# Attention on one core: some projections computed in halves over two steps, the others moved

## Chip, cores and metric

The kernel runs on one core of a Trainium2 chip. The metric is the device time of one execution in microseconds, taken as the median of several runs.

## The reference

The input is x, 8 sequences of 512 rows of 512 numbers, float32 throughout. A layer of attention and a gated layer stand one after the other, each between two layer normalisations and with a residual:

```python
x = x + layernorm(attention(layernorm(x)))
x = x + layernorm(ffn(layernorm(x)))
# attention: 16 heads of 32
c_kv = x @ W_dkv + b_dkv                  # 512 -> 128 ("ckv")
v = c_kv @ W_uv + b_uv                    # values
c_q = x @ W_dq + b_dq                     # 512 -> 128 ("cq")
q = rotary(c_q @ W_qr + b_qr)             # queries
k = rotary(x @ W_kr + b_kr)               # keys
out = softmax(q k^T / sqrt(32)) v @ W_o + b_o
# ffn: Hadamard transform, up and gate projection, silu, Hadamard transform, W_down
```

## The kernel before

The kernel has two phases. Attention takes the first 916 us of the profiled execution and the gated layer the rest. The change touches attention alone.

**Work by batches and steps.** A batch is one of the 8 sequences (number b). Its 16 heads form 4 groups of 4, and its 512 keys 4 chunks of 128, so that a batch has 16 steps i = 4 x group + c, and attention 128 steps t. The loop over t stands in the source in the order in which each engine then works; no scheduler reorders it. In every step PE does the following:

1. `scores_t(n, c)`: two tiles t (each 128 x 1024, two banks of PSUM) with the transposed scores of one key chunk for the four heads of group n. First come four short bfloat16 matmuls that lay down the rows' biases (L564), then four float32 ones of queries and keys (L573). ACT turns each tile into exponentials p (L585).
2. `weigh` of the step before: exponentials by values, into ops (L606).
3. In the last step of a group (i = 3, 7, 11, 15) `bias_rows` of the next group: four small transposes ps_b (L550), which ACT copies; the second exponential of such a step stands behind that copy.
4. In the third step of a group (i = 2, 6, 10, 14) `sums`: the columns of the exponentials are added up, into l (L623).
5. A piece of the table `BETWEEN`, if the step has one.
6. `row_max` for the step six steps later: two tiles s (L527), of which DVE takes maxima (L535).
7. Another piece, of the table `BEHIND`.

The pieces prepare the next batch (offset 1 in a table's entry), the one after (2), the present one (0) or finish the last (-1): `x_flip` transposes normalised x into xT; `compress` makes cq or ckv from xT by four matmuls of 512 columns; `key` makes one of four key blocks by four such matmuls; `query` and `value` make a block by one matmul each; `out_proj` makes a block of the output by five; `fold` applies a 128 x 128 Hadamard matrix to a sixteenth of W_down by one matmul. `fold_load` reads that sixteenth from memory, DVE does four further levels of the transform in later steps (`levels`), and a DMA writes it back. The steps in `FOLDS` do a fold, those in `READ` load one.

**What keys and queries need afterwards.** ACT copies the product with its bias into lin (L416). At the next call of `turn`, in the step that follows, DVE shuffles lin into rot (L420) and POOL does two products and a sum (L421 to L423). POOL also adds up pairs of exponentials in the second and fourth step of each group (`add_up`, L594), splits the maxima (`split`), takes powers of variances (`inverse_std`, L104 and L105) and adds residuals (L694). DVE adds the pairs' sums in each group's first step (`add_pairs`, L599).

**Buffers.** [...] The pool ps_s has three tiles of two banks, tag s, which `row_max` and `scores_t` take in turn: s, s, t, t in each step. One bank belongs to ops. One bank, ps_f with tag f, serves everything else: bias rows, sums, transposes and all pieces, one after the other. `bank(wide, name)` gives a piece a tile of ps_s if `wide` is set and the bank f otherwise:

```python
if wide or end:
    return ps_s.tile([P, 2, S], F32, tag="s", name=name)[:, 0, :]
return ps_f.tile([P, S], F32, tag="f", name=name)
```

In the steps of `TWO` the piece of `BETWEEN` is not done ahead of `row_max` but behind it, just ahead of the piece of `BEHIND`, and with `wide` set. The first batch has tables of its own (`FIRST_BETWEEN`, `FIRST_BEHIND`), since part of its work is done before the loop and nothing has to be finished. The last batch does the first steps of the gated layer's input instead of preparing a successor (`ENTRY`, `in_step`: fxt, L195, and fxh, L207).

Over the steps, `early` and `later` place the normalisation of x (ACT), its load (SP, step 4), statistics (DVE, steps 6 to 9) and shift (DVE, step 11), and the output's statistics, shift, residual and store.

The pieces of a batch before, by step (in the tables of all batches but the first):

| step | ahead of row_max | behind row_max |
|---|---|---|
| 0, 1 | x_flip 1, x_flip 2 | value 2, key 3 |
| 2, 3 | | query 3, value 3 |
| 4 | x_flip 3 | fold |
| 5, 6 | | cq, key 0 |
| 7 | | out_proj 0 |
| 8, 9, 10 | | query 0 + out_proj 1, query 1 + out_proj 2, fold + out_proj 3 |
| 11, 12 | | key 1, query 2 + ckv |
| 13 | x_flip 0 | value 0 |
| 14, 15 | | key 2, value 1 |

Of the kernel before, what the change touches and what calls it, by code (L numbers as in the profile page):

```python
# [10 lines left out]
F32 = mybir.dt.float32  # L11
BF16 = mybir.dt.bfloat16
I32 = mybir.dt.int32
AF = mybir.ActivationFunctionType
# [3 lines left out]
P = 128  # L18
NB, S, D = 8, 512, 512
DH, GH = 32, 4  # L20
NK = D // P
NT = S // P
INTER = 2048
NI = INTER // P
# [4 lines left out]
C_BDKV, C_BDQ, C_BKR, C_BQR = 0, 1, 2, 6  # L29
# [4 lines left out]
def sandwich_kernel(  # L34
# [19 lines left out]
    nc = tc.nc  # L54
# [17 lines left out]
    pv = const.tile([P, C_END], F32, name="pv")  # L72
    nc.gpsimd.dma_start(out=pv, in_=pvec)
    h128 = const.tile([P, P], F32, name="h128")
# [18 lines left out]
    qkv = ctx.enter_context(tc.tile_pool(name="a_qkv", bufs=2))  # L93
# [148 lines left out]
    with ExitStack() as actx:  # L242
        wa = actx.enter_context(tc.tile_pool(name="wa", bufs=1))
        row = actx.enter_context(tc.tile_pool(name="a_row", bufs=4))
        cproj = actx.enter_context(tc.tile_pool(name="a_c", bufs=1))
        rp = actx.enter_context(tc.tile_pool(name="a_rope", bufs=3))
        pp = actx.enter_context(tc.tile_pool(name="a_p", bufs=1))
        fo = actx.enter_context(tc.tile_pool(name="a_fold", bufs=1))
# [41 lines left out]
        wdkv_sb = wa.tile([P, NK, P], F32, name="wdkv_sb")  # L290
        wdq_sb = wa.tile([P, NK, P], F32, name="wdq_sb")
# [26 lines left out]
        def bank(wide, name):  # L318
# [3 lines that stand above are left out]
# [60 lines left out]
        def x_norm(b, t):  # L382
            rs, sh = stats[b]
            xn[b, t] = row.tile([P, D], F32, tag="xn", name=f"xn_{b}_{t}", bufs=3)
            nc.scalar.activation(
                xn[b, t], xs[b][:, t, :], AF.Identity, bias=sh[:, t : t + 1], scale=rs[:, t : t + 1]
            )
# [26 lines left out]
        def rotate(dst, ps, bias, scale, name, first=None, second=None):  # L414
            lin = rp.tile([P, S], F32, tag="lin", name=f"lin_{name}")
            nc.scalar.activation(lin, ps, AF.Identity, bias=bias, scale=scale)  # L416

            def rest():
                rot = rp.tile([P, S], F32, tag="rot", name=f"rot_{name}", bufs=2)
                nc.vector.stream_shuffle(rot, lin, swap)  # L420
                (first or nc.gpsimd).tensor_mul(lin, lin, cs[:, 0, :])  # L421
                (second or nc.gpsimd).tensor_mul(rot, rot, cs[:, 1, :])
                (first or nc.gpsimd).tensor_add(dst, lin, rot)  # L423

            turns.append(rest)
# [53 lines left out]
            )  # L479
            folds.append((n, w))  # L480

        def fold(n, wide=False):
            _, w = folds.pop(0)
            ps = bank(wide, f"fd_{n}").rearrange("p (c m) -> p c m", c=NI)
            nc.tensor.matmul(ps, lhsT=h128, rhs=w, start=True, stop=True)
            z = fo.tile([P, NI, NF], F32, tag="z", name=f"fz_{n}")
            a = fo.tile([P, NI, NF], F32, tag="a", name=f"fa_{n}")
            nc.scalar.copy(z, ps)

            def level(src, dst, h):  # L490
                sv = src.rearrange("p (a t b) n -> p a t (b n)", t=2, b=h)
                dv = dst.rearrange("p (a t b) n -> p a t (b n)", t=2, b=h)
                nc.vector.tensor_add(dv[:, :, 0, :], sv[:, :, 0, :], sv[:, :, 1, :])
                nc.vector.tensor_sub(dv[:, :, 1, :], sv[:, :, 0, :], sv[:, :, 1, :])

            def keep():
                nc.sync.dma_start(
                    out=wdd.rearrange("p (c m) -> p c m", c=NI)[:, :, ts(n, NF)], in_=w
                )

            levels.extend(
                [
                    lambda: level(z, a, 1),
                    lambda: level(a, z, 2),
                    lambda: level(z, a, 4),
                    lambda: level(a, w, 8),
                    keep,
                ]
            )

        levels = []


        brow, nms, pt, o_ps, o_sb, rec = {}, {}, {}, {}, {}, {}
# [245 lines left out]
        for t in range(3):  # L760
# [11 lines left out]


        BETWEEN = {
            0: (x_flip, 1, 1), 1: (x_flip, 1, 2), 4: (x_flip, 1, 3),
            8: (query, 1, 0), 9: (query, 1, 1), 12: (query, 1, 2), 13: (x_flip, 2, 0),
        }
        BEHIND = {
            0: (value, 0, 2), 1: (key, 0, 3), 2: (query, 0, 3), 3: (value, 0, 3),
            5: (compress, 1, "cq"), 6: (key, 1, 0), 7: (out_proj, -1, 0),  # L780
            8: (out_proj, -1, 1), 9: (out_proj, -1, 2), 10: (out_proj, -1, 3),
            11: (key, 1, 1), 12: (compress, 1, "ckv"), 13: (value, 1, 0), 14: (key, 1, 2),
            15: (value, 1, 1),
        }

        FIRST_BETWEEN = {i: p for i, p in BETWEEN.items() if i not in (8, 9)}
        FIRST_BEHIND = {
            **BEHIND, 7: (query, 1, 0), 8: (None, NB, None), 9: (key, 1, 1),
            10: (None, NB, None), 11: (query, 1, 1),
        }  # L790
        OUT = {7: 0, 8: 1, 9: 2, 10: 3}

        APART = {n: (0, 2) for n in range(NG - NK, NG - 2)}
        APART[NG - 2], APART[NG - 1] = (0, 2, 3), (0, 1, 2, 3)

        FOLDS = [4, 10, 15] + [NK * NT * b + i for b in range(1, NB - 1) for i in (4, 10)]
        FOLDS.append(NK * NT * (NB - 1) + 1)
        READ = [0] + [g - 3 for g in FOLDS[1:]]


        TWO = (8, 9, 10, 12, 15)

        def piece(table, b, i, wide=False):
            if b == 0 and table is BEHIND and i == 8:
                out_bias()
            pieces = table if b else FIRST_BETWEEN if table is BETWEEN else FIRST_BEHIND
            if i in pieces:
                fn, d, what = pieces[i]
                if 0 <= b + d < NB:
                    fn(b + d, what, *([True] if wide else []))  # L810
            at = NK * NT * b + i
            if at in FOLDS and (table is BETWEEN) == (b > 0 and i in TWO or i == 15 or b == NB - 1):
                fold(FOLDS.index(at), wide)
            if b == NB - 1 and (i, table is BEHIND) in ENTRY:
                in_step(*ENTRY[i, table is BEHIND], 2 * NT)

# [17 lines left out]
        def early(b, i):  # L834

            if b > 0 and i - 3 in OUT:
                residual(b - 1, OUT[i - 3])
            if b + 2 < NB and i in (12, 14, 15):
                x_norm(b + 2, max(i - 13, 0))
            if i == 0 and 0 < b + 1 < NB:  # L840
                x_norm(b + 1, 3)

        def later(b, i):

            if b > 0 and i - 1 in OUT:
                out_stats(b - 1, OUT[i - 1])
            if b > 0 and i - 2 in OUT:
                out_shift(b - 1, OUT[i - 2])
            if b > 0 and i - 5 in OUT:
                store(b - 1, OUT[i - 5])  # L850
            if b + 2 < NB:
                if i == 4:
                    load_x(b + 2, NT)
                elif 6 <= i < 10:
                    x_stats(b + 2, i - 6)
                elif i == 11:
                    x_shift(b + 2)

        for t in range(NG * NT):
# [755 lines left out]
```

## Time and profile before

| what | value |
|---|---|
| median of 3 runs | 2101.72 us (2101.01 to 2101.88) |
| profiled execution | 2102.66 us, span 2100.9 us |
| granted TensorE clock | 0.999 |
| attention, from the first step to the gated layer | 46.8 to 916.3 us |
| batch 0 | 102.1 us |
| each of batches 1 to 5 | 108.6 to 108.7 us |
| batch 6 | 108.1 us |
| last batch and end of attention | 116.0 us |

The lengths of the batches are those of the windows in which I asked the trace for busy time; each begins with the first bias matmul (L564) of a batch. PE is TensorE's matmuls and PEld its loads of weights, DVE is VectorE, ACT ScalarE, POOL GpSimd and SP the engine that issues DMAs. A float32 matmul appears as two instructions in the trace, so a key block of four matmuls is "x8". The lengths of single matmuls include a tail of the pipeline in which the next one already runs; the chain of waits gives the time from one to the next.

### The profile page before, as it was taken

How to read it: one execution, taken by the hardware profiler on the slowest of the kernel's cores; microseconds unless marked ns; L12 is line 12 of the kernel's file. 1: busy time of each engine (PE TensorE's matmuls, PEld its weight loads, DVE VectorE, ACT ScalarE, POOL GpSimd, SP SyncE). 2: the span in 40 equal slices, each digit the busy share in tenths (PEclk: the TensorE clock that was granted, in tenths of full speed). 3: DMA queues.
4: the chain of work that ended last, by engine and by line, in shares of the span. 5: the costliest groups of instructions: out<-in, count | busy, mean ns of one | idle time of the engine just before them, and what ended most of it. 6: DMA issues, size and time to landing. Idle time of an engine off the chain costs nothing.

```text
span 2100.9 us, 26741 instructions
## 1 busy us (share of the span) xinstructions
PE 2076.8 (99%) x9035; PEld 1057.4 (50%) x9042; DVE 1414.4 (67%) x2356; ACT 745.3 (35%) x1199; POOL 1575.4 (75%) x1629
## 2 busy tenths in 40 slices
PE   8999999999999999999999999999999999999998
PEld 4333333333333333344444677676676766777753
DVE  5698777676767677465545866678866678656542
ACT  3554545555555545522121122222222222222211
POOL 4787979787878889645453678788888879787852
PEclk9999999999999999999999999999999999999999
DMA  3112121212121122237454444444343344444432
GB/s 122 37 31 51 42 54 49 47 51 52 46 57 46 32 66 72 70 104 221 145 166 152 146 143 148 133 138 149 130 157 131 131 137 144 138 158 136 138 112 70
DMA packets 215913, 218.12 MB, mean 104 GB/s; under 512 B 87376, under 2 KB 147920, under 8 KB 215776
## 3 DMA queue, kind: packets, MB, share of 16 engines
q1 hardware_dynamic: 215424, 215.32, 33.2%
q8 instruction: 72, 1.18, 0.2%
q0 software_dynamic: 352, 1.08, 0.1%
q14 instruction: 65, 0.53, 0.1%
HBM read 169.18 MB, written 46.92 MB: 103 GB/s over the span
## 4 chain that ended last, share of the span: by engine, by line
PE 94%; DVE 3%; issue 1%; POOL 1%; ACT 1%; DMA 0%; SPq 0%; POOLq 0%; DVEq 0%; ACTq 0%
PE d L1123 24%; PE psy L1225 18%; PE s L527 6%; PE ops L606 6%; PE ps_k L439 5%; PE ps_y L662 5%; PE t L573 5%; PE u L1106 5%; PE g L1106 4%; PE psz L1516 3%; PE t L564 3%; PE l L623 2%; PE ps_q L454 2%; PE ps_v L466 1%; PE ps_cq L407 1%; PE fxh L207 1%
## 5 line engine op out<-in xcount | busy, mean ns | idle before, releaser
L1225 PE MATMUL psy<-wd,g 128*128 128x512 f32 x896 | 448.9, 592 | 0.0
L535 DVE TENSOR_REDUCE nm<-s 128x2 f32<-128x1024 f32 x256 | 300.8, 1216 | 175.1 <-PE s L527 175.1
L1347 POOL TENSOR_TENSOR pr<-pr,pr 128x512 f32<-128x512 f32 x294 | 391.6, 1357 | 9.0
L594 POOL TENSOR_TENSOR p<-p,p 128x512 f32<-128x512 f32 x244 | 330.2, 1384 | 22.1 <-PE ops L606 22.1
L585 ACT ACTIVATE p<-t 128x1024 f32<-128x1024 f32 x256 | 251.8, 1023 | 89.0 <-PE t L573 89.0
L1123 PE MATMUL d<-xb,wq 128*128 128x256 f32 x992 | 254.2, 380 | 1.9 <-DVE inner L1139 1.4
L1123 PEld LDWEIGHTS d<-tt,wq 128*128 128x128 f32 x864 | 164.0, 190 | 144.4 <-issue 106.0
L1123 PE MATMUL d<-tt,wq 128*128 128x256 f32 x864 | 233.8, 379 | 0.2 <-DVE pr L1144 0.2
L1140 POOL TENSOR_TENSOR pr<-inner 128x256 f32<-128x256 f32 x168 | 126.0, 750 | 138.5 <-DVE inner L1139 105.9
L1123 PEld LDWEIGHTS d<-xb,wq 128*128 128x128 f32 x992 | 186.7, 190 | 62.4 <-issue 30.1
L1225 PEld LDWEIGHTS psy<-wd,g 128*128 128x128 f32 x896 | 169.7, 190 | 49.3 <-issue 29.4
L1136 ACT COPY inner<-d 128x256 f32<-128x256 f32 x168 | 62.6, 373 | 309.6 <-PE d L1123 291.5
L1132 ACT COPY inner<-d 128x256 f32<-128x256 f32 x168 | 62.6, 372 | 300.3 <-PE d L1123 193.2
L527 PE MATMUL s<-kT,qT 32*128 32x512 f32 x1024 | 153.8, 639 | 0.7 <-DVE nm L535 0.7
L573 PE MATMUL t<-qT,kT 32*128 32x512 f32 x1024 | 142.8, 598 | 0.0
L606 PE MATMUL ops<-p,v 128*32 128x512 f32 x1024 | 136.8, 605 | 0.0
L1142 POOL TENSOR_TENSOR pr<-pr,inner 128x256 f32<-128x256 f32 x168 | 136.5, 813 | 0.0
L1123 PE MATMUL d<-T,wq 128*128 128x256 f32 x496 | 127.6, 380 | 0.2
L1144 DVE TENSOR_TENSOR pr<-d,inner 128x256 f32<-128x256 f32 x168 | 70.5, 420 | 75.5 <-PE d L1123 72.9
L439 PE MATMUL ps_k<-xT,wkr_sb 128*128 128x512 f32 x256 | 118.3, 605 | 0.7 <-ACT xT L397 0.7
L662 PE MATMUL ps_y<-wo_sb,oT 128*128 128x512 f32 x256 | 115.8, 593 | 0.9 <-DVE oT L657 0.6
L1135 DVE TENSOR_TENSOR inner<-d,inner 128x256 f32<-128x256 f32 x168 | 70.5, 419 | 62.4 <-PE d L1123 62.0
(219 smaller groups left out, 3263.8 us busy)
## 6 DMA issues: line engine op xcount, KB each, us to landing
wq<-wdeep SPq DMA_DIRECT2D x168, 448.0 KB, 4.2
wd<-wdd SPq DMA_DIRECT2D x112, 256.0 KB, 2.8
wdeep<-w SPq DMA_DIRECT2D x32, 448.0 KB, 5.5
xr<-in_x SPq DMA_DIRECT2D x32, 256.0 KB, 2.8
xin<-x1d SPq DMA_DIRECT2D x32, 256.0 KB, 4.0
xres<-x1d SPq DMA_DIRECT2D x32, 256.0 KB, 3.3
out<-fy SPq DMA_DIRECT2D x32, 256.0 KB, 2.0
rec<-rd SPq DMA_DIRECT2D x124, 64.0 KB, 2.0
```

The lines of the kernel that those rows point to most:

```text
L439: nc.tensor.matmul(ps, lhsT=wkr_sb[:, k, ts(g, P)], rhs=xT[b][:, k, :], start=(k == 0), stop=(k == NK - 1),)
L527: nc.tensor.matmul(sp[j // 2][:, j % 2, :], lhsT=qT[b][rows, g, ts(qc, P)], rhs=kT[b][rows, g, :], start=True, stop=True,)
L535: nc.vector.tensor_reduce(nms[n][:, qc, 2 * h : 2 * h + 2], sp[h], AX.X, ALU.max, negate=True)
L573: nc.tensor.matmul(sp[j // 2][:, j % 2, :], lhsT=kT[b][rows, g, ts(c, P)], rhs=qT[b][rows, g, :], start=False, stop=True,)
L585: nc.scalar.activation(pt[n, c, h], sp[h], AF.Exp)
L594: nc.gpsimd.tensor_add(into, into, pt[n, c, j // 2][:, j % 2, :])
L606: nc.tensor.matmul(o_ps[n][j * DH : (j + 1) * DH, :], lhsT=vv[b][:, c, ds(g * P + j * DH, DH)], rhs=pt[n, c, j // 2][:, j % 2, :], start=( ...
L662: nc.tensor.matmul(ps, lhsT=oT[b][:, k, ts(qc, P)], rhs=wo_sb[:, k, :], start=False, stop=(k == NK - 1),)
L1106: nc.tensor.matmul(ps, lhsT=w[:, SLOT[n], k, :], rhs=rhs[:, k, :], start=k == 0, stop=k == 1)
L1123: nc.tensor.matmul(ps, lhsT=w[:, INNER[m]], rhs=rhs[m], start=True, stop=True)
L1225: nc.tensor.matmul(ys_[t], lhsT=g[:, ts(t, P)], rhs=w, start=n == 0, stop=n == NI - 1)
L1347: nc.gpsimd.tensor_add(pr[n][:, h], pr[a][:, h], pr[b][:, h])
```

## The change

In every batch but parts of the first and last, the pieces are laid out anew:

| steps | ahead of row_max | behind row_max |
|---|---|---|
| 15 and 0 | x_flip 2 (step 0) | halves of value 1 and key 3 |
| 1 and 2 | x_flip 3 (step 1) | halves of value 2 and cq |
| 3 and 4 | | halves of value 3 and key 0 |
| 5 and 6 | | halves of a fold and key 1 |
| 7, 8, 9, 10 | | query 0 to 3, each with out_proj 0 to 3 |
| 11 and 12 | x_flip 0 (step 12) | halves of a fold and ckv |
| 13 and 14 | x_flip 1 (step 13) | halves of value 0 and key 2 |

`halves` takes the one bank f for a step. Its first 256 columns hold one half of the small piece (one matmul of 256 columns), the other 256 one half of the large piece (four such matmuls); then ACT copies the two out one after the other. After the second half the key's rotation or the fold's levels are queued as before. Where only one piece of a pair is left, in the last batch, it is done whole in the first of the two steps.

The normalisation of x moves from steps 12, 14, 15 to 11, 12, 14, its shift from 11 to 10, the loads of the folds by one step. `TWO` is now 7, 8, 9, 10, 15. In the first batch halves begin at step 13; queries 1, 2 and 3 are done in steps 9, 11 and 10. In the last batch value 2 is done in step 1 and the fold in step 2.

```diff
         def rotate(dst, ps, bias, scale, name, first=None, second=None):
             lin = rp.tile([P, S], F32, tag="lin", name=f"lin_{name}")
             nc.scalar.activation(lin, ps, AF.Identity, bias=bias, scale=scale)
+            rotation(dst, lin, name, first, second)
+
+        def rotation(dst, lin, name, first=None, second=None):
             def rest():
...
+        HC = S // 2
+        split_in_two = {}
+
+        def half(h, ps, fn, b, what):
+            cols = ts(h, HC)
+            if fn is fold:
...
+                nc.tensor.matmul(pv_, lhsT=h128, rhs=w[:, blocks, :], start=True, stop=True)
+                def leave():
+                    nc.scalar.copy(z[:, blocks, :], pv_)
+                    if h == 1:
+                        folds.pop(0)
+                        fold_levels(n, w, z)
+                return leave
+            if fn is value:
...
+                nc.tensor.matmul(
+                    ps, lhsT=cT[b, "ckv"][:, ts(what, P)], rhs=wuv_sb[:, cols], start=True, stop=True
+                )
+                return lambda: nc.scalar.copy(vv[b][:, what, cols], ps)
...
+            for k in range(NK):
+                nc.tensor.matmul(
+                    ps, lhsT=w[:, k, :], rhs=xT[b][:, k, cols], start=k == 0, stop=k == NK - 1
+                )
+            def leave():
+                nc.scalar.activation(dst[:, cols], ps, AF.Identity, bias=bias)
+                if fn is key and h == 1:
+                    rotation(kT[b][:, what, :], dst, f"k{b}_{what}")
+            return leave
...
         BETWEEN = {
-            0: (x_flip, 1, 1), 1: (x_flip, 1, 2), 4: (x_flip, 1, 3),
-            8: (query, 1, 0), 9: (query, 1, 1), 12: (query, 1, 2), 13: (x_flip, 2, 0),
+            0: (x_flip, 1, 2), 1: (x_flip, 1, 3), 7: (query, 1, 0), 8: (query, 1, 1),
+            9: (query, 1, 2), 10: (query, 1, 3), 12: (x_flip, 2, 0), 13: (x_flip, 2, 1),
         }
-        BEHIND = {
+        BEHIND = {7: (out_proj, -1, 0), 8: (out_proj, -1, 1), 9: (out_proj, -1, 2), 10: (out_proj, -1, 3)}
+        HALVES = {
+            15: ((value, 1, 1), (key, 1, 3)), 1: ((value, 0, 2), (compress, 1, "cq")),
+            3: ((value, 0, 3), (key, 1, 0)), 5: ((fold, 0, None), (key, 1, 1)),
+            11: ((fold, 0, None), (compress, 1, "ckv")), 13: ((value, 1, 0), (key, 1, 2)),
+        }
+        FIRST_BETWEEN = {
+            0: (x_flip, 1, 1), 1: (x_flip, 1, 2), 4: (x_flip, 1, 3), 9: (query, 1, 1),
+            10: (query, 1, 3), 12: (x_flip, 2, 0), 13: (x_flip, 2, 1),
+        }
+        FIRST_BEHIND = {
             0: (value, 0, 2), 1: (key, 0, 3), 2: (query, 0, 3), 3: (value, 0, 3),
...
+            5: (compress, 1, "cq"), 6: (key, 1, 0), 7: (query, 1, 0), 9: (key, 1, 1),
+            11: (query, 1, 2), 12: (compress, 1, "ckv"),
+        }
...
-        FOLDS = [4, 10, 15] + [NK * NT * b + i for b in range(1, NB - 1) for i in (4, 10)]
-        FOLDS.append(NK * NT * (NB - 1) + 1)
-        READ = [0] + [g - 3 for g in FOLDS[1:]]
-        TWO = (8, 9, 10, 12, 15)
+        FOLDS = [4, 10, 15, NK * NT * (NB - 1) + 2]
+        READ = [0, 7, 12]
+        READ += [NK * NT * b + i for b in range(1, NB - 1) for i in (2, 8)]
+        READ.append(NK * NT * (NB - 1) - 1)
+        TWO = (7, 8, 9, 10, 15)
+
+        def halves(b, i):
+            for first, h in ((i, 0), ((i - 1) % (NK * NT), 1)):
+                if first not in HALVES or b == 0 and i < 13:
+                    continue
...
+                ps = bank(False, f"ps_{live[1][0].__name__}_{live[1][1]}_{live[1][2]}_{h}")
+                for leave in [half(h, ps[:, ts(n, HC)], *which) for n, which in enumerate(live)]:
+                    leave()
...
+            if table is BEHIND:
+                halves(b, i)
...
-            if b + 2 < NB and i in (12, 14, 15):
-                x_norm(b + 2, max(i - 13, 0))
+            if b + 2 < NB and i in (11, 12, 14):
+                x_norm(b + 2, (11, 12, 14).index(i))
...
-                elif i == 11:
+                elif i == 10:
                     x_shift(b + 2)
```

## The prediction

> **What bounds the kernel now.** I read the page's first part, then busy time by windows, one per batch of attention, then the chain of waits.
>
> ```profile
> PE 2076.8 (99%) x9035; PEld 1057.4 (50%) x9042; DVE 1414.4 (67%) x2356; ACT 745.3 (35%) x1199; POOL 1575.4 (75%) x1629
> 46.80:148.90 102.10, 98.48 (x577) 32.82 (x578) 79.73 (x97) 52.94 (x68) 82.44 (x79) 1.00 0.13 30
> 257.50:366.20 108.70, 108.65 (x618) 37.17 (x619) 83.71 (x106) 57.83 (x77) 90.53 (x90) 1.00 0.19 50
> ```
>
> After the window's length stand PE, PEld, DVE, ACT and POOL. In batches 1 to 6 PE is busy in all but 0.05 us; POOL comes next with 90.5 of 108.7. So PE sets the pace, but a busy record can hide a wait. The chain shows where (start, length, instruction):
>
> ```profile
> 265.88 1.07 PE s L527 x8
> 266.95 3.63 PE ps_k L439 x8
> 270.58 0.33 PE t L564 x4
> 270.91 0.86 PE t L573 x8
> ...
> 273.62 1.07 PE s L527 x8
> 274.70 1.05 PE ps_q L454 x2
> 275.75 0.65 PE t L564 x4
> 276.40 0.86 PE t L573 x8
> ```
>
> The same four matmuls of t take 0.33 behind a long piece (ps_k) and 0.65 behind a short one (ps_q). The reader is to see that 0.32 us is a wait: t's second tile takes the buffer of the step's first s tile, which DVE must have reduced.
>
> ```profile
> 266.99 2.36 DVE L535 TENSOR_REDUCE nm<-s 128x2 f32<-128x1024 f32 x2 [0.59 <-PE s L527]
> ```
>
> DVE starts 1.11 after s (265.88 to 266.99) and one reduction takes 1.22, so the buffer is free 2.35 to 2.4 after s began. A short piece puts t 1.07+1.06 = 2.1 behind s, a long one 4.7. In this batch six steps are late: 0, 1, 3, 4, 5 and 14, each behind a short piece in the step before.
>
> **What the skill says.** "TensorE: Matmul & The Clock Gate" (Wait — 56ns, not 53.3ns?) prices a matmul at its columns by 2.4 GHz plus 2.5 ns. The trace agrees for equal passes: a float32 matmul is two passes, seven passes of 256 columns (L1123) take 1199.63 to 1201.14, 0.216 each, and two of 512 (L1225) 0.86 to 1202.00, 0.43 each. Halving costs 2 ns per pair. "TensorEngine Tiling (Array Packing)" (Key Properties) says that changing the tiling mode drains the engine: ps_k's 8 passes at 0.43 leave 0.20 of 3.63, ps_v's two 0.20 of 1.06. I take 0.21 per block; it is not paid between a value half and a key half, both 128x128. "PSUM — Partial Sum Buffer" (PSUM bank collisions raise a hardware error) asks to guard PSUM by bank. No run here shows it, but the compiled order agrees: the small half's copy on ACT waits for the last key matmul of the block.
>
> **The change, part by part.** The compiled order of both kernels gives counts: DVE, POOL and SP issue the same instructions; PE gets 76 half blocks (26 key, 6 cq, 6 ckv, each twice) in place of 38 long and 38 short pieces, and ACT 76 evictions more. SP's fold loads move by one step (1 and 7 to 2 and 8); the fold reads them three steps later as before. The load of x stays at step 4; its statistics follow in step 6, after some 11.6 us where 12.6 were.
>
> *Half blocks, one batch of 1 to 5.* Ten passes, 10 x 0.216 + 0.21 = 2.37. Twelve are 28.4. They replace five long pieces at 3.63, one at 3.53 (behind a query), five short at 1.06 and one at 0.96: 27.9. **+0.5.**
>
> *Late t.* s now lies 1.07+2.37 = 3.44 ahead of t, against 2.4 needed. 6 x 0.32: **-1.9.** It rests on DVE starting in time. I added up its queue step by step: with add_pairs (2.35 in steps 0, 4, 8, 12) and fold levels (up to 1.9) it is at most 0.4 late against 1.0 of slack.
>
> *Queries.* They go from 2, 8, 9, 12 to 7, 8, 9, 10. In 8 and 9 nothing changes, in 10 a query takes the fold's place (0.96 both). Step 7 also makes bias rows, where the second exp follows the copy of the rows. The query takes the s buffer which that exp frees:
>
> ```profile
> 581.98 1.03 ACT L585 ACTIVATE p<-t 128x1024 f32<-128x1024 f32 x1
> 582.46 0.30 PEld L466 LDWEIGHTS ps_v<-wuv_sb,ckv 128*128 128x128 f32 x2 [0.76 <-ACT brow L554]
> 146.98 1.12 PE L485 MATMUL fd<-fw,h 128*128 128x512 f32 x2 [0.53 <-ACT p L585]
> ```
>
> The first two lines are step 15 of batch 4: exp ends at 583.01, but PE is ready at 582.46. That is 0.6 with the semaphore. The third is the one place before where a piece takes an s buffer in such a step (the fold of batch 0's step 15): PE sat idle 0.53 for just this exp. Queries by chain: 1.06+1.18+0.96+0.96 before, 0.96+0.6+1.18+0.96+0.96 after. **+0.5**, and queued behind the waiting query is the output projection of its step.
>
> *x transposes* keep 0.59 each; steps without work ahead of s (1.25 against 1.07, s waits for an exp) are 4, 5, 8, 9 instead of 5, 8, 9, 12. **0.** Normalisations, shift and statistics of x move with them on ACT and DVE, hidden as now; if ACT is late, the transposes wait.
>
> *Evictions.* A 512-column copy is 0.587, one of 256 (L212) 0.373; 688 ns for the biased form gives an estimate of 0.47. Both halves end by 0.97 after t starts, exp starts at 1.35. **0**; were ACT 0.4 later, exp and then s would slip.
>
> Sum -0.9; adding the 16 steps row by row gives 107.9 against 108.67, -0.77. I take **-0.8**, five times; batch 6 the same (two statistics more on DVE cost 0.2, two missing transposes no less): **-4.8**.
>
> *Batch 0.* There the first step table moves query 3 to step 10 and queries 1 and 2 to 9 and 11; no halves before 13. POOL must rotate q1, k1 and q3 ahead of step 11's additions (before: k1 alone):
>
> ```profile
> 113.74 1.02 POOL L105 TENSOR_TENSOR rs_x<-rs_x,nhalf 128x4 f32<-128x4 f32 x1
> 114.73 1.27 POOL L421 TENSOR_TENSOR lin_k<-lin_k,cs 128x512 f32<-128x512 f32 x1
> ...
> 119.06 5.38 POOL L594 TENSOR_TENSOR p<-p,p 128x512 f32<-128x512 f32 x4
> ```
>
> A rotation is three of these, 4.1 to 4.4. From 114.8, three end at 127.3 and the additions at 132.7 instead of 124.4. DVE's add_pairs of step 12 waits for them, then a level and a bias operation; step 13's reductions start near 136.3, t of step 14 at 137.8. After that: t 1.3, ops and l 1.85, s 1.07, half 2.37 give 144.3; step 15 with bias rows, fold (its 0.6 again) and a half 7.4: 151.7, where 148.9 stood. PE work taken over from batch 1 is in it. Bounds: 0 if POOL's rotations overlap better, +4 with rotations as slow as q0's here (5.7). **+2.6.**
>
> *Batch 7.* Key 3 and query 3 leave it (-3.63, -1.06), a half (2.37) replaces value 2 in step 0 and value 2 replaces the key. Waits of 0.6 (s of step 0, for DVE) and 0.85 (t of step 1) go; new ones come in step 2 (the fold waits about 0.85 for the copy of l in the one free bank) and step 3 (no piece ahead of t: 1.3). Steps 0 to 6: 39.9 against 41.2. **-1.3.** The rest keeps its instructions: 0.
>
> Together **-3.5**. The profiled execution took 2102.66 (span 2100.9 and 1.8 around it), 0.9 above the median of 2101.72: 2099.2 on its terms, **2098.2** as a median. 0.2% is 4.2 us, about what a measurement of this kernel can tell from no change.
>
> **Rivals.**
> *Faster: the new waits are hidden.* Step 7's 0.6 in six batches and batch 0's 2.6 vanish: -9.7, **2092.0**. For it: PE's slack is repaid in many places. Against: both waits stand in the trace.
> *Slower: POOL's queue reaches PE.* Four rotations now follow each other in steps 8 to 11, among additions and residuals:
>
> ```profile
> 425.83 0.19 POOL L104 TENSOR_TENSOR rs_y<-mvy,eps 128x1 f32<-128x1 f32 x1 [5.10 <-DVE mvy L100]
> 427.29 1.27 POOL L421 TENSOR_TENSOR lin_q<-lin_q,cs 128x512 f32<-128x512 f32 x1 [0.64 <-DVE rot_q L420]
> ```
>
> The first query's rotation fits into the 5.1 us that POOL now waits. The others push step 11's additions to 47 us after step 7 starts and the last rs_y to 49.3; in step 12 DVE waits for both ahead of step 13's reductions, due at 50.2, with 1.0 more until t is held. Each us beyond some 1.7 costs PE one per batch. q0 of batch 0 took 5.7 instead of 4.0; two such rotations make +3.4, a stall of 1.7, less 0.8 gained: six times 0.9, plus batch 0's bound of 4, less batch 7's 1.3: +8.1, **2109.8**. It decides from 2.1 us of delay, where the same sum is nothing.
> *The change does not do what it says.* If a half block drained once inside (+0.1), 76 blocks give +7.6, **2105.8**; if t stayed late all the same, 6 x 1.9 is missing: 2109.6.
>
> **How the numbers follow.** Forecast 0.55, own range 2095.5 to 2101, of which 0.12 lies under 2097.5; hidden waits 0.31; POOL 0.08; halves dear 0.06, half of it over 2105.9. Faster 0.43, same 0.46, slower 0.11. The range leaves out about 0.1 at each end: 2091.5 (the hidden waits' own half us below 2092.0) to 2104.5.
>
> **What would show it.** Right: the four bias matmuls of t at 0.33 in steps 0 to 5 and 14 of the chain; half blocks at 2.37 from the value's first pass to t; the query of step 7 behind an exp; batches 1 to 5 at 107.9; batch 0 some 3 longer; batch 7 shorter. Wrong: half blocks over 2.45, t at 0.65 or more, POOL busy without a gap through steps 8 to 15 with DVE idle ahead of add_pairs, or batches at 107.3 and less.

## The result: 0.2% slower

The changed kernel takes 2106.66 us in the median (11 runs, 2105.83 to 2107.40), the kernel before in the same comparison 2101.88 (11 runs); the ratio is 1.0022, with a 95% interval of 1.0013 to 1.0032. The forecast was 2098.2. The profiled execution of the changed kernel took 2106.66 with a span of 2104.5, against 2102.66 and 2100.9.

Line numbers below are those of the changed kernel: t is L626 (biases) and L635, ops L668, l L685, s L589, the value half L546, the key half L564, DVE's reductions L597, add_pairs L661, POOL's additions L656, its rotations L424 to L426, its powers of variances L104 and L105, its residuals L756. A fold level is the two operations L499 and L500. The page's first part, and busy time by windows for batch 0 and batch 2 (the columns as before: length, PE, PEld, DVE, ACT, POOL, granted clock, DMA share, GB/s):

```profile
PE 2072.4 (98%) x9422; PEld 1127.2 (54%) x9422; DVE 1404.1 (67%) x2356; ACT 754.6 (36%) x1275; POOL 1561.5 (74%) x1629
45.51:156.50 110.99, 103.78 (x600) 37.45 (x600) 82.57 (x100) 54.27 (x72) 88.07 (x82) 0.97 0.12 27
264.97:373.38 108.41, 107.58 (x678) 48.14 (x679) 78.20 (x102) 59.28 (x88) 88.48 (x91) 1.00 0.20 50
```

PE does 4.4 us less than before, and the span is longer: the rest is idle. Batch 0 has 7.2 us in which PE stands still (before: 3.6), and its granted clock is 0.97; a batch of the steady part, formerly idle for 0.05, now is for 0.83. By lengths:

| part | before | after | difference | forecast |
|---|---|---|---|---|
| start of the first step | 46.78 | 45.51 | -1.3 | 0 |
| batch 0 | 102.11 | 110.99 | +8.9 | +2.6 |
| batch 1 | 108.62 | 108.47 | -0.15 | -0.8 |
| batches 2 to 5, each | 108.67 | 108.41 | -0.26 | -0.8 |
| batch 6 | 108.09 | 107.57 | -0.5 | -0.8 |
| batch 7, to its last t | 90.24 | 88.26 | -2.0 | -1.3 |

The sum is +3.9; the spans of the two executions differ by 3.6, for what follows is 0.3 shorter. The start is no part of the change: in the runs below it lies between 45.0 and 46.2, whatever was edited. Without it the parts add up to +5.2.

**The steady part.** The chain of waits through step 0 of batch 2 (start, length, instruction):

```profile
265.04 0.33 PE t L626 x4
265.36 0.86 PE t L635 x8
266.22 1.00 PE ops L668 x8
267.22 0.59 PE xt L394 x4
267.81 1.07 PE s L589 x8
268.87 0.63 PE ps_key L546 x2
269.50 1.73 PE ps_key L564 x8
271.23 0.33 PE t L626 x4
```

A value half and a key half take 268.87 to 271.23, 2.36, and the biases of t behind them 0.33: the late t is gone, here and in steps 1, 3, 4 and 5. The chain comes to step 14 of batch 2 by another way:

```profile
357.78 1.13 POOL rs_y L104
...
359.00 0.55 POOL rs_y L105
...
359.58 0.21 DVE sh_y L112
359.79 1.14 DVE nm L597
...
360.98 0.39 PE t L626 x2
```

The reader is to see that PE is not the first in this row: t of step 14 starts when DVE has reduced s of step 13, DVE when it has formed sh_y, and this when POOL has taken the power of the last variance. That power is the last in POOL's queue behind four rotations, step 11's additions and a residual. POOL's timeline one batch later (batch 3) shows how long two of these take:

```profile
439.65 5.33 POOL L656 TENSOR_TENSOR p<-p,p 128x512 f32<-128x512 f32 x4
...
446.32 0.19 POOL L104 TENSOR_TENSOR rs_y<-mvy,eps 128x1 f32<-128x1 f32 x1
...
458.84 6.12 POOL L656 TENSOR_TENSOR p<-p,p 128x512 f32<-128x512 f32 x4
...
466.14 1.17 POOL L104 TENSOR_TENSOR rs_y<-mvy,eps 128x1 f32<-128x1 f32 x1
```

The additions of step 9 take 5.33, those of step 11 6.12; one power takes 0.19, the last 1.17. Step 14 lasts 7.15 instead of the 6.47 that it takes without this wait (in the runs q3_at_4 and best2 below).

**Batch 0.** The chain through its step 14, and the clock beside it (the windows as above):

```profile
131.84 2.27 DVE p L661
134.12 1.41 DVE fz L499
135.52 1.40 DVE fz L500
136.93 1.67 DVE bo_in L365
138.59 1.15 DVE nm L597
...
139.78 0.61 PE t L626 x2
140.39 1.71 PE t L635 x8
142.10 1.86 PE ops L668 x8
143.96 1.71 PE l L685 x8
```

```profile
134.00:139.78 5.78, 0.71 (x4) 0.10 (x3) 5.78 (x6) 0.75 (x2) 5.70 (x5) 0.93 0.00 0
139.78:148.50 8.72, 8.72 (x42) 3.30 (x42) 4.88 (x6) 3.23 (x4) 3.97 (x7) 0.65 0.01 0
```

Two things are to be seen. First, between the late add_pairs and the reductions DVE spends 4.5 us on a fold level and a bias operation (L365), and POOL is busy throughout. The kernel before needed 1.3 for them, while POOL stood still (its own line numbers):

```profile
131.16 0.41 DVE L493 TENSOR_TENSOR fz<-fa 128x256 f32<-128x256 f32 x1
131.50 0.41 DVE L494 TENSOR_TENSOR fz<-fa 128x256 f32<-128x256 f32 x1
131.84 0.68 DVE L365 TENSOR_TENSOR bo_in<-bo_in,bo_hi 128x512 f32<-128x512 f32 x1
133.24 1.26 POOL L421 TENSOR_TENSOR lin_q<-lin_q,cs 128x512 f32<-128x512 f32 x1 [3.08 <-DVE rot_q L420]
```

Second, when PE starts after 5 us of idling, t takes 1.71 where it takes 0.86 elsewhere, ops 1.86 for 1.00, l 1.71 for 0.86: the granted clock is 0.65 in this stretch. So part of the stall is paid a second time.

### The profile page after: what moved, and what is told of

It reads as the page before. It is cut to its first block, busy times and chain, and to the rows that moved or that the text cites. A ratio compares the mean times of both kernels' runs of the same rounds, so it can differ in the third digit from the quotient of the medians.

```text
span 2104.5 us, 27594 instructions
## 1 busy us (share of the span) xinstructions
PE 2072.4 (98%) x9422; PEld 1127.2 (54%) x9422; DVE 1404.1 (67%) x2356; ACT 754.6 (36%) x1275; POOL 1561.5 (74%) x1629
## 4 chain that ended last, share of the span: by engine, by line
PE 85%; POOL 7%; DVE 5%; issue 1%; ACT 1%; DMA 0%; POOLq 0%; SPq 0%; DVEq 0%; ACTq 0%
PE d L1216 24%; PE psy L1318 18%; PE s L589 5%; PE ops L668 5%; PE u L1199 5%; PE g L1199 4%; PE t L635 4%; PE ps_key L564 4%; POOL p L656 3%; PE ps_y L724 3%; PE psz L1609 3%; PE t L626 2%; DVE nm L597 1%; PE l L685 1%; PE fxh L207 1%
## 5 line engine op out<-in xcount | busy, mean ns | idle before, releaser
L597 DVE TENSOR_REDUCE nm<-s 128x2 f32<-128x1024 f32 x256 | 301.0, 1217 | 207.0 <-PE s L589 207.0
L656 POOL TENSOR_TENSOR p<-p,p 128x512 f32<-128x512 f32 x244 | 322.5, 1352 | 11.4 <-PE ops L668 6.2
L1318 PEld LDWEIGHTS psy<-wd,g 128*128 128x128 f32 x896 | 169.7, 190 | 49.3 <-issue 29.7
L589 PE MATMUL s<-kT,qT 32*128 32x512 f32 x1024 | 154.6, 640 | 0.7 <-DVE nm L597 0.7
L668 PE MATMUL ops<-p,v 128*32 128x512 f32 x1024 | 137.7, 608 | 0.0
L635 PE MATMUL t<-qT,kT 32*128 32x512 f32 x1024 | 137.1, 595 | 0.0
L424 POOL TENSOR_TENSOR lin_k<-lin_k,cs 128x512 f32<-128x512 f32 x32 | 45.1, 1409 | 106.8 <-DVE rot_k L423 106.8
```

What stands on the lines that cost most here:

```text
L589: nc.tensor.matmul(sp[j // 2][:, j % 2, :], lhsT=qT[b][rows, g, ts(qc, P)], rhs=kT[b][rows, g, :], start=True, stop=True,)
L597: nc.vector.tensor_reduce(nms[n][:, qc, 2 * h : 2 * h + 2], sp[h], AX.X, ALU.max, negate=True)
L635: nc.tensor.matmul(sp[j // 2][:, j % 2, :], lhsT=kT[b][rows, g, ts(c, P)], rhs=qT[b][rows, g, :], start=False, stop=True,)
L656: nc.gpsimd.tensor_add(into, into, pt[n, c, j // 2][:, j % 2, :])
L668: nc.tensor.matmul(o_ps[n][j * DH : (j + 1) * DH, :], lhsT=vv[b][:, c, ds(g * P + j * DH, DH)], rhs=pt[n, c, j // 2][:, j % 2, :], start=( ...
L1318: nc.tensor.matmul(ys_[t], lhsT=g[:, ts(t, P)], rhs=w, start=n == 0, stop=n == NI - 1)
```

## Experiments

My theory after this comparison: batch 0 is long since POOL makes three rotations ahead of step 11's additions and DVE follows late; the lowered clock adds 2.9; and in the steady part POOL's fourth rotation gives back what the halves gain. Rivals: the half blocks and transposes of steps 13 to 15 themselves, slow matmuls for another reason, DVE's own operations. In each run a step counts from the first bias matmul of its t to the next one.

### first_q3 and first_old: fewer rotations ahead of the additions

Both take query 3 of batch 1 out of step 10 of batch 0 and put it into step 0 of batch 1. first_old moves the others too:

```diff
-            0: (x_flip, 1, 1), 1: (x_flip, 1, 2), 4: (x_flip, 1, 3), 9: (query, 1, 1),
-            10: (query, 1, 3), 12: (x_flip, 2, 0), 13: (x_flip, 2, 1),
+            0: (x_flip, 1, 1), 1: (x_flip, 1, 2), 4: (x_flip, 1, 3),
+            12: (query, 1, 2), 13: (x_flip, 2, 0), 14: (x_flip, 2, 1),
...
-            11: (query, 1, 2), 12: (compress, 1, "ckv"),
+            11: (query, 1, 1), 12: (compress, 1, "ckv"),
...
+            if table is BEHIND and b == 1 and i == 0:
+                query(1, 3)
```

> The changed kernel, but query 3 of batch 1 leaves step 10 of batch 0 for step 0 of batch 1. POOL theory: POOL rotates two pieces instead of three ahead of step 11's additions, so these end 4.1 us earlier (127.7 instead of 131.8), DVE's add_pairs and the reductions of step 13 follow, and TensorE no longer idles 5 us ahead of t of step 14, so its clock stays up too: batch 0 lasts 102.5 to 104 (110.99 in the changed kernel), of which 1.06 is only the query that moves into batch 1; the whole -6 to -8 us, near 2099.5. Rival, batch 0 is longer because of its steps 13 to 15 themselves (half blocks, x transposes): batch 0 near 109.9, the whole 2106.5.

> The changed kernel with the rotations of batch 0 as they were: k1 alone ahead of step 11's additions, query 1 in step 11, query 2 in step 12, query 3 in step 0 of batch 1, the x transposes of batch 2 in steps 13 and 14. POOL theory by the dose: the additions end near 124, batch 0 lasts 100.5 to 102, the whole -7.5 to -9 us (2098 to 2099); if 4 us of delay are already hidden, no better than with two rotations ahead. Rival, steps 13 to 15 themselves: batch 0 near 109.9, the whole 2106.5.

Measured: 2109.46 (ratio 1.0034, 1.0021 to 1.0047) and 2108.93 (1.0034, 1.0021 to 1.0047), no better than the change itself (1.0022). Batch 0 takes 108.1 and 108.4, so it is 2.6 to 2.9 shorter, 1.06 of it the query; but in both the stall stays and the clock falls. (From the first bias matmul of step 14 to its first score matmul, called "t's biases" from here on, 4.13 and 4.46 pass instead of 5.46; a step without a wait has 0.23, the kernel before has 1.67 here.) Batch 1 loses more than batch 0 gains: 5.5 and 3.9. The dose says that my theory was too simple: in first_old the additions end at 123.1, long before DVE wants them at 126.9, and t is late all the same. DVE and POOL of first_old in this stretch, by the timeline (start, length, engine, instruction):

```profile
126.94 4.33 DVE L661 TENSOR_TENSOR p<-p,p 128x1024 f32<-128x1024 f32 x2
131.19 1.49 DVE L499 TENSOR_TENSOR fz<-fa 128x256 f32<-128x256 f32 x1
132.60 1.48 DVE L500 TENSOR_TENSOR fz<-fa 128x256 f32<-128x256 f32 x1
134.00 1.74 DVE L365 TENSOR_TENSOR bo_in<-bo_in,bo_hi 128x512 f32<-128x512 f32 x1
```

```profile
127.93 2.26 POOL L424 TENSOR_TENSOR lin_q<-lin_q,cs 128x512 f32<-128x512 f32 x1
130.15 2.25 POOL L425 TENSOR_TENSOR rot_q<-rot_q,cs 128x512 f32<-128x512 f32 x1
132.47 1.32 POOL L426 TENSOR_TENSOR qT<-lin_q,rot_q 128x512 f32<-128x512 f32 x1
133.76 5.74 POOL L656 TENSOR_TENSOR p<-p,p 128x512 f32<-128x512 f32 x4
```

The two engines hold each other up: while POOL rotates without a gap, DVE's operations on two tiles of SBUF take 1.49 instead of the 0.41 of the kernel before, and POOL's 2.25 instead of 1.27. The other place for query 3 costs as well: with it in step 0 of batch 1, POOL's splitting of the maxima comes late and step 3's bias rows wait 1.9 us for it (ops 2.93 instead of 1.00; in first_q3 the clock falls after it once more, in first_old it does not), and step 0 pays 2.0 for the query.

### filler: PE kept at work through the stall

```diff
+            if b == 0 and i == 13:
+                ps = bank(False, "filler")
+                for _ in range(5):
+                    nc.tensor.matmul(ps, lhsT=h128, rhs=wuv_sb, start=True, stop=True)
```

> The changed kernel with five float32 matmuls of 512 columns (4.3 us, their result is not used) between the half block of step 13 of batch 0 and t of step 14, where TensorE is idle for 5 us. Clock theory: t still waits for the reductions of step 13, to 139.5 to 140.5, but t, ops and l then take 0.86, 1.00 and 0.86 instead of 1.71, 1.86 and 1.71, and s 1.07: batch 0 is 2.5 to 3.2 us shorter (108.1), the whole near 2103.7. Rival, the slow matmuls come from something else (POOL or DVE beside them): no change, or up to 0.5 longer, 2106.7 to 2107.

Measured: 2104.22 (20 runs, 2103.32 to 2106.87; ratio 1.0012, 1.0006 to 1.0019), batch 0 at 108.15. Timeline of PE, and the clock:

```profile
135.08 4.56 PE L1026 MATMUL filler<-wuv_sb,h 128*128 128x512 f32 x10 [0.84 <-ACT lin_k L569]
139.57 0.44 PE L626 MATMUL t<-brow,ones_b 32*128 32x512 bf16 x4
139.79 1.07 PE L635 MATMUL t<-qT,kT 32*128 32x512 f32 x8
140.80 1.06 PE L668 MATMUL ops<-p,v 128*32 128x512 f32 x8
```

```profile
139.50:148.50 9.00, 9.00 (x71) 3.82 (x70) 8.05 (x13) 5.01 (x7) 4.36 (x9) 1.00 0.06 9
```

t begins at the same 139.8, but what follows has its usual length, at a clock of 1.00. So 2.8 us of batch 0 are the clock, and idling causes it. The Trainium skill states this in "TensorE: Matmul & The Clock Gate" (What's actually happening): after an idle window of about 3.4 us the array runs at half its clock. The traces agree for the idle stretches of 3.74 to 6.57 us ahead of t of step 14 (first_q3, first_old, the changed kernel and the next run); shorter ones are met below.

### before_first: batch 0's order alone, in the kernel before

```diff
-        FIRST_BETWEEN = {i: p for i, p in BETWEEN.items() if i not in (8, 9)}
+        FIRST_BETWEEN = {i: p for i, p in BETWEEN.items() if i not in (8, 9, 12)}
+        FIRST_BETWEEN.update({9: (query, 1, 1), 10: (query, 1, 3)})
...
-            10: (None, NB, None), 11: (query, 1, 1),
+            10: (None, NB, None), 11: (query, 1, 2),
```

Query 3 is also taken out of step 2 of batch 1 (`if i in pieces and not (b == 1 and table is BEHIND and i == 2)`).

> The kernel before, whole pieces everywhere, with one thing of the change: queries 1, 3 and 2 of batch 1 in steps 9, 10 and 11 of batch 0 (before: 1 in step 11, 2 in step 12, 3 in step 2 of batch 1). POOL theory: three rotations ahead of step 11's additions, a stall of 4 to 6 us ahead of t of step 14 and a lowered clock after it: batch 0 108 to 111 instead of 102.1 (1.06 of it query 3, which leaves batch 1), the whole +5 to +8, 2107 to 2110. Rival, the order of the queries is harmless by itself and only the half blocks with it are slow: batch 0 103.2 to 104, the whole 2101.5 to 2103.

Measured: 2109.36 (ratio 1.0038, 1.0025 to 1.0051); batch 0 takes 109.73, 7.6 more, t of step 14 comes after 6.57 us of idling, and from its first score matmul to ops 2.24 pass, as many as in the changed kernel. DVE's three operations take 1.48, 1.48 and 1.74 there too. The order of three queries is enough, with no half block in the kernel: the rival of steps 13 to 15 falls.

### dve_light and gap: is it DVE beside POOL?

dve_light keeps the fold level and the bias operation out of step 12 of batch 0:

```diff
-            if levels and (c > 0 or 0 < i and b < 1):
+            held = b == 0 and i == 12
+            if levels and (c > 0 or 0 < i and b < 1) and not held:
                 levels.pop(0)()
-            if small:
+            if small and not held:
```

gap is first_old with query 2 behind the s of step 12 instead of ahead of it, and query 3 behind that of step 14 instead of in batch 1:

```diff
+        FIRST_TWO = (8, 9, 10, 12, 15)
...
-            if not last_steps and (i not in TWO or b == NB - 1):
+            if not last_steps and (i not in (TWO if b else FIRST_TWO) or b == NB - 1):
                 piece(BETWEEN, b, i)
...
+            if b == 0 and i == 14:
+                query(1, 3, True)
-            if i in TWO and b < NB - 1:
+            if i in (TWO if b else FIRST_TWO) and b < NB - 1:
                 piece(BETWEEN, b, i, True)
```

> The changed kernel; in step 12 of batch 0 DVE takes no fold level and no operation of the output bias (L499, L500 and L365, 1.48, 1.48 and 1.74 there); they follow one step later each. Theory, DVE is held by POOL: its two-input operations take 1.48 beside a busy POOL and 0.41 beside an idle one, and these 4.5 us, not the late additions alone, make the stall: the reductions of step 13 start near 134.1 instead of 138.5, t of step 14 waits about 1 us instead of 5.5, the clock stays up; batch 0 103.5 to 104.5 (110.99), the whole -6.5 to -7.5, near 2099.5. Rival, the additions alone decide: the stall shrinks by at most the 1.5 us that the three take without POOL beside them; batch 0 near 109.5 with the clock still lowered. Second rival: the three operations, a step later, are as slow and hold t of step 15 instead; batch 0 106 to 108.

> The changed kernel with batch 0's rotations in exactly the order of the kernel before up to step 12: query 1 behind step 11, query 2 behind the s of step 12 (in an s buffer), so that POOL waits for DVE's shuffle of query 2 and stands still during step 12's add_pairs and fold level; query 3 comes in step 14. Theory, DVE is held by POOL: as in the kernel before the level takes 0.41 each and the bias operation 0.68, reductions of step 13 start near 132 to 133, t of step 14 waits 0.5 to 1.7, no clock drop; batch 0 102.5 to 104, of which 1.06 is query 3; the whole -7 to -8.5, 2098 to 2100. Rival, it was not POOL's order (with query 2 a little earlier in the step the stall stayed at 4.46): batch 0 near 108.5, the whole 2106 to 2108.

Measured: dve_light 2103.57 (ratio 1.0009, 1.0001 to 1.0018), batch 0 at 103.78 with the additions as late as in the changed kernel (131.75). t's biases take 0.97 instead of 5.46 and the clock stays. Of the stall, 4.5 us thus go with the three operations, and only 0.7 (0.97 less the usual 0.23) are left with the additions alone. The gain in batch 0 is half lost in batch 1 (111.89, +3.4), where the fold's copy must wait for the levels that now lag by one; I had not thought of it:

```profile
188.52 0.37 ACT L537 COPY fz<-ps_key 128x256 f32<-128x256 f32 x1 [5.21 <-DVE fa L500]
```

gap takes 2100.65 (12 runs; ratio 0.9995, 0.9986 to 1.0004), batch 0 at 103.70. Its timelines of DVE and of POOL beside those of first_old above:

```profile
130.43 0.41 DVE L499 TENSOR_TENSOR fz<-fa 128x256 f32<-128x256 f32 x1
130.76 0.41 DVE L500 TENSOR_TENSOR fz<-fa 128x256 f32<-128x256 f32 x1
131.10 0.68 DVE L365 TENSOR_TENSOR bo_in<-bo_in,bo_hi 128x512 f32<-128x512 f32 x1
```

```profile
127.27 2.14 POOL L426 TENSOR_TENSOR qT<-lin_q,rot_q 128x512 f32<-128x512 f32 x1
132.50 1.27 POOL L424 TENSOR_TENSOR lin_q<-lin_q,cs 128x512 f32<-128x512 f32 x1 [3.09 <-DVE rot_q L423]
```

The same operations on tiles of the same shape: 0.41 while POOL waits 3.09 us for DVE's shuffle, 1.49 while it works. "SBUF — State Buffer" (Who interferes with whom) of the Trainium skill names the reason: a DVE operation with two SBUF inputs and a reading POOL operation need the same port, whole instruction by whole instruction. The numbers fit, for 1.49 is about 0.41 and most of one POOL product of 1.27, and the reductions of s (one input) stay at 2.28 to 2.36 for two with POOL busy or not. That the port is the reason is what the page states; the runs show that POOL's work beside them is. Not every operation with one input is spared, either: L350 takes 0.41 at 114.61 of first_old and 1.49 at 137.36 of the kernel before, with POOL busy at both. POOL's gap in the kernel before came from the place of query 2: POOL waits there for a shuffle that stands behind the three operations in DVE's queue. This is what the change took away.

### step7, q3_at_4 and q0_at_3: the steady part

step7 puts the output projection of step 7 ahead of the query:

```diff
+            late = i == 7 and 0 < b
+            if late:
+                piece(BEHIND, b, i)
             if i in TWO and b < NB - 1:
                 piece(BETWEEN, b, i, True)
-            piece(BEHIND, b, i)
+            if not late:
+                piece(BEHIND, b, i)
```

q3_at_4 moves query 3 from step 10 to step 4, and q0_at_3 query 0 from step 7 to the end of step 3:

```diff
-            if g == 0:
+            if b not in qT:
                 qT[b] = qkv.tile([P, NK, S], F32, tag="qT", name=f"qT_{b}")
...
-            9: (query, 1, 2), 10: (query, 1, 3), 12: (x_flip, 2, 0), 13: (x_flip, 2, 1),
+            9: (query, 1, 2), 4: (query, 1, 3), 12: (x_flip, 2, 0), 13: (x_flip, 2, 1),
```

```diff
-            0: (x_flip, 1, 2), 1: (x_flip, 1, 3), 7: (query, 1, 0), 8: (query, 1, 1),
+            0: (x_flip, 1, 2), 1: (x_flip, 1, 3), 8: (query, 1, 1),
...
                 halves(b, i)
+                if b and i == 3 and b + 1 < NB:
+                    query(b + 1, 0, True)
```

> The changed kernel; in step 7 of batches 1 to 6 the output projection goes ahead of the query. Theory: the query's 0.6 wait for the second exp vanishes behind the projection, s 1.67 becomes 1.07: -0.6 in each of six batches, -3.6, 2103.1. Rival: the query's rotation starts 3.6 us later on POOL, joins the queue of steps 8 to 12, and the wait of step 14 grows by as much: 0.

> The changed kernel; from batch 1 on query 3 goes from step 10 to step 4, so that POOL has three rotations in steps 8 to 11 instead of four. POOL theory: the additions of step 11 and the inverse deviation of step 12 come 4 us earlier, t of step 14 no longer waits (0.23 and 0.96 instead of 0.68 and 1.17; in batch 6 in step 13): -0.66 in each of six batches, some 0.1 lost to the query's longer form, -3 to -4, 2102.6 to 2103.6. Rival: DVE waits there for the inverse deviations and residuals, which stay: 0, or +0.5 where the query in step 4 holds the one free bank.

> The changed kernel; from batch 1 on query 0 leaves step 7 for the end of step 3, behind the half block, so that its rotation comes first on POOL in step 4, where POOL stands still for 7.2 us ahead of k0's rotation. POOL theory: three rotations instead of four in steps 8 to 11 take the wait from t of step 14 (7.15 becomes 6.47; batch 6: 6.45 becomes 5.79), and unlike query 3 in step 4, whose rotation came behind k0's and held the split of step 5 and the bias rows of step 7, this one fits into the gap; the 0.6 wait of step 7 goes too; one drain of the query is saved or paid (0.2). -1.2 to -1.5 in each of six batches, -7 to -9, 2098 to 2099.5; batch 0 stays at 111. Rival: any further rotation ahead of step 5 holds the split, and step 7 pays 3 us a batch again: 2115 to 2125.

Measured: step7 2105.33 (20 runs; ratio 1.0015, 1.0008 to 1.0021). Step 7 takes 8.20 instead of 8.89, and step 14 7.81 instead of 7.15, so a batch is as long as it was (108.38). The chain of step7 in batch 2 shows why:

```profile
357.75 1.13 POOL rs_y L104
...
360.94 0.39 PE t L626 x2
```

The power comes at 357.75 where it came at 357.78 in the changed kernel. POOL's queue sets this moment, and what PE saves ahead of it only lengthens PE's wait. Batch 6 alone kept 1.2, which is nearly all of the 1.3 between the two medians.

q3_at_4: 2128.33 (ratio 1.0126, 1.0109 to 1.0143). The wait of step 14 is gone as expected (6.47 in batches 1 to 5), so query 3's rotation was its cause; but step 7 takes 11.6 to 13.9. POOL in batch 3:

```profile
420.21 5.46 POOL L656 TENSOR_TENSOR p<-p,p 128x512 f32<-128x512 f32 x4
...
426.86 0.25 POOL L607 CAST parts<-nm 128x16 bf16<-128x16 f32 x1
```

Two rotations, the additions and then the split of the maxima follow each other, and the split ends at 427.1, while PE has been ready for the bias rows since 424.5. In five of six batches, though not in this one, the clock falls after this wait of only 2.7 to 2.9 us, too (0.64 to 0.80 through the rest of the step, which then takes up to 2.3 us more). Here the measurement is below the skill's 3.4, and it decides. Nor is the length of the wait all that counts: in step 3 of batch 1 the clock fell after 1.86 us in first_q3 and stayed after 1.88 in first_old.

q0_at_3: 2101.23 (ratio 0.9995, 0.9987 to 1.0004), batches 2 to 5 at 107.63, 0.77 less than in the changed kernel, not the 1.2 to 1.5 expected. Its rotation fits into POOL's gap and step 7 loses its wait; but step 14 still takes 7.06. q3_at_4 also took one of the four rotations away, the last, and step 14 was free: the number of rotations in steps 8 to 11 is not what counts.

### best and best2: both repairs

best is gap with q0_at_3. best2 has the queries one step earlier: 0 at the end of step 3, 1 in step 7 behind the projection, 2 and 3 in steps 8 and 9.

```diff
-            0: (x_flip, 1, 2), 1: (x_flip, 1, 3), 8: (query, 1, 1),
-            9: (query, 1, 2), 10: (query, 1, 3), 12: (x_flip, 2, 0), 13: (x_flip, 2, 1),
+            0: (x_flip, 1, 2), 1: (x_flip, 1, 3), 7: (query, 1, 1), 8: (query, 1, 2),
+            9: (query, 1, 3), 12: (x_flip, 2, 0), 13: (x_flip, 2, 1),
...
```

> Both repairs: batch 0's rotations as in the run named gap, query 0 at the end of step 3 from batch 1 on. If the two causes are separate, the gains add: 2100.7 (gap) less 1.2 to 1.5 in each of six batches is 2091.5 to 2093.5, under both kernels by 0.4%. Rival: they share POOL's queue in batch 1, where query 3's late rotation already holds step 3 by 1.0: 2093.5 to 2096.

> The run named best with its queries one step earlier: query 0 at the end of step 3, query 1 in step 7 behind the output projection, 2 and 3 in steps 8 and 9, none in step 10. In best, with query 0 gone from step 7, t of step 14 still waited 0.61. POOL theory, refined: not the number of rotations in steps 8 to 11 decides but the one that lies right ahead of step 11's additions (query 3, of step 10); without it step 14 takes 6.47 instead of 7.07, -0.6 to -0.7 in each of batches 1 to 5, -3 to -4: 2091.5 to 2092.5. Rival: three rotations are still in steps 8 to 10 and POOL's queue carries over, as in the run named step7: 2095 to 2096.

Measured: best 2095.56 (ratio 0.9969, 0.9957 to 0.9980), best2 2093.19 (0.9961, 0.9948 to 0.9975), so both are faster than the kernel before, by 0.3 and 0.4%. best lies 2 us above what was expected, where the rival had put it, but not for the rival's reason: batch 1 gains as much as the others. The gains of the two repairs add: against gap, best gains 0.6 to 1.0 in each of batches 1 to 6, as q0_at_3 does against the changed kernel; the rest that the expectation counted on is step 14, still at 7.07, and batch 1 still pays 1.0 in step 3 for query 3. In best2 step 14 takes 6.47. A steady batch of best2 by windows:

```profile
257.22:364.16 106.94, 106.94 (x678) 48.04 (x678) 80.59 (x102) 59.45 (x88) 89.75 (x91) 1.00 0.20 51
```

PE is busy in all of it. best2 moves three queries at once; with q3_at_4 and q0_at_3 it shows that what mattered was the rotation right ahead of step 11's additions. It still misses the range expected by 0.7: batches 6 and 7 are slower than in the changed kernel, by 0.1 and 0.4 (in steps 13, 14 and 3); I did not follow that up.

## Why the prediction was wrong, by its own steps

- **Half blocks, late t, transposes, evictions:** right, but for the late t of step 14. A half block takes 2.36 (2.37 forecast); t's biases take 0.33 in the chain in the five other steps that were late; the transposes take 0.59, and PE stands still in steps 7 and 14 only (0.53 and 0.30 in batch 2), so evictions delay nothing.
- **Queries:** right. In step 7 s lasts 1.67, the 0.6 wait that the step 15 of the kernel before had shown. Removing it alone brought nothing, for the reason in the next point.
- **Batches 1 to 5, -0.8 each:** the step that failed is the zero for step 14. Without its wait of 0.68 a batch would be at 107.73, against 107.9 forecast. I had this wait as a rival and counted POOL's operations at their undisturbed length: counted from the start of step 7, the additions were to end at 47 and the last power at 49.3. In batch 3 they end at 48.6 and 51.6. Step 11's additions took 6.12 instead of 5.33, and the last power's first operation 1.17 instead of 0.19, both beside DVE's add_pairs. The rival, to which I gave 0.08, had the mechanism (POOL's queue reaches PE) but not the size: it put a stall of 1.7 and +0.9 a batch, where 0.68 and -0.26 were measured; in number -0.8 was nearer. Batch 6 (-0.5) loses in step 13, which takes 6.45; step7 has 5.79 there. That the rival's total, 2109.8, lies nearer to 2106.66 than 2098.2 does is luck: batch 0 made up for it.
- **Batch 0, +2.6, in truth +8.9:** the place was right and the first term also: counted from the start of the batch the additions end at 86.3 (85.9 forecast). The term that failed is "then a level and a bias operation": I had taken them at the 1.3 us that they take with POOL idle, and a busy POOL makes them 4.5, so the reductions start 3.5 later than forecast and t 3.3. A second term is missing from the sum: I let PE resume at full clock after the stall, and t, ops and l at half clock cost 2.8 more. The two make 6.1, which is all that is missing: the forecast's own times give 151.7 - 148.9 = +2.8, not the +2.6 written there. Batch 0 is thus most of the 7.4 by which the sum over all parts missed.
- **Batch 7, -1.3, in truth -2.0:** its new waits are where I put them (PE idles 0.78 ahead of the fold in step 2, 0.85 forecast, and 1.11 ahead of t's second tile in step 3). Steps 0 to 6 take 39.2 instead of the 39.9 forecast; which term is 0.7 too large I did not look for.
- **The upper bound of the range:** +4 for batch 0 was to take in rotations as slow as q0's. It let POOL be slow beside DVE and forgot that DVE is then slow beside POOL.

## What to carry to other kernels

An operation that moves to another place in its own queue also changes what the other engines run beside: price it by rows where its neighbours are as busy as they will be, not by the fastest row. When PE will wait for several us, add the matmuls behind the wait at half clock: here this happened after every wait of 3.7 us and more, after five of six of 2.7 to 2.9, and after one of two of 1.9. And before taking a wait away, ask which engine sets the moment at which the next one ends; in a stretch that POOL paces, time saved on PE comes back as a longer wait.

## What I had not expected of the hardware

- DVE operations of 0.41 us on two SBUF tiles take 1.48 beside a busy POOL and 0.41 in its gap, and the slowing goes both ways (POOL's product 2.25 instead of 1.27).
- After 5 us without matmuls the clock was 0.65 over the next 8.7 us, with matmuls at half speed for about 6 of them. Waits of 2.7 to 2.9 us were enough in five batches of six, and one of 1.86 us was; none of 1.6 us or less was in the attention of these runs.
